# A two-layer graph attention kernel: layer 2's factor rows leave TensorE, and its node steps are put at other places

## The chip, the core and the metric

The kernel runs on one NeuronCore of a Trainium2 chip. The metric is the device time of one execution in microseconds (us). The engines are PE (TensorE), DVE (VectorE), ACT (ScalarE), POOL (GpSimd) and SP (SyncE, which only issues transfers). PSUM is the accumulator memory that PE writes, eight banks of 2 KB a partition; DVE and ACT can read and write it too. SBUF is the working memory.

## What is computed

Two graph attention layers and a small dense network over N = 6250 nodes and 100,000 edges (plus one self loop a node), edges sorted by destination; the result is added to the input `x`.

```python
def gat_conv(x, src, dst, W, a_src, a_dst, bias, heads):
    h = (x @ W).reshape(n, heads, -1)
    alpha_s = (h * a_src[None]).sum(-1); alpha_d = (h * a_dst[None]).sum(-1)
    e = leaky_relu(alpha_s[src] + alpha_d[dst], 0.2)
    alpha = softmax of e over the edges of one dst
    return segment_sum(h[src] * alpha[:, :, None], dst).reshape(n, -1) + bias

h = maximum(layernorm(x), 0)
h = relu(gat_conv(h, ..., W1, heads=4))      # layer 1, 768 -> 256
h = relu(gat_conv(h, ..., W2, heads=1))      # layer 2, 256 -> 256
h = relu(h @ Wm1 + bm1)                      # 256 -> 256
out = x + (h @ Wm2 + bm2)                    # 256 -> 768
```

## The kernel before

Nodes are cut into 49 tiles of 128 (`NT`). Edges are cut into tiles of 128, four to a group; there are 196 groups (`NG`) and 98 pairs of groups (`NU`). So one node tile corresponds to four groups, or two pairs, or eight half groups. The change lies in layer 2 (about 1425 to 2570 us of the profiled span).

One group of layer 2, two halves of two edge tiles each:

- POOL issues four indirect transfers (L726, `G<-table,src_i`), each of which gathers the rows of 128 source nodes into one quarter of a buffer `G`. There are ten such buffers, and POOL is let eight groups ahead (`AHEAD`). A buffer is free again when PE has read it.
- DVE makes a one-hot matrix for the whole group (L751, 128x512), and for each half multiplies and takes the larger (L825, L827, into the scratch tensor `iota_ps`), and multiplies that into the one-hot (L828). L825 reads a *factor row*: one number for each of the 128 destination nodes of a pair of groups, the same on all partitions. It lies in PSUM as `rho_ps`.
- PE multiplies the four edge tiles' rows by the four weighted one-hots (L834, `o_ps`, summed over a pair of groups).
- After each pair DVE adds the sum to what came over from the pair before (L852, `acc`), and ACT moves the part that reaches into the next window (L861, `sum`, two instructions).

The factor rows are made on PE: `meet(t)` (L767) turns a column of `win` into a row on all partitions, two for each node tile, into two PSUM banks of their own, used in turn.

When a node tile has its sum, a Python generator `steps` (L1205 ff.) does the rest of it, a piece at a time: DVE finishes the sum (L1203, L1204 `all_`, L1215 `rden`), ACT scales it (L1218, `o`), PE turns it (L1038, `tp`), ACT adds the bias (L1044, `rT`), PE multiplies by Wm1 (L1227, four matmuls into the second half of `tp`), ACT (L1232, `mT`), PE puts the bias row into `y_ps` (L1165) and multiplies by Wm2 (L1237), DVE adds the input (L1241, `y`, twice, 384 columns each), SP stores (L1266). Both halves of `y` use one `y_ps` bank one after the other, so the products of the second half wait until DVE has added the first.

The kernel issues everything in an order written out by hand: each engine runs its instructions in the order in which the loop over groups `g` writes them, and waits only on semaphores. Two tables set the places of layer 2: `UP_AT` (the half group at which a pair's rows are summed up) and `STEPS_AT` (the half groups at which a tile's generator is moved on one `yield`). For most tiles the six places are

```python
STEPS_AT = {t: [8 * t + 19 + k for k in (1, 2, 5, 8, 11, 14)] for t in range(NT - 2)}
```

so a tile's generator is advanced over 14 half groups, and two tiles are in work at a time.

PSUM has the eight banks: `iota_ps` (one), tag "n" (two: `tp`, `y_ps` and the completed rows `missing`/`missing2` take turns), tag "o" (three: `o_ps`), "factors" (one) and "parts" (one), the last two holding the `rho_ps` rows in layer 2. A semaphore wait is set wherever two engines touch the same PSUM tensor, whichever part of it.

Ten groups of source rows are not gathered in time from memory but completed on the chip (`next_missing`, L417/L419 on PE, `next_whole`, L423 on ACT).

Of the kernel before, what the change touches and what calls it, by code (L numbers as in the profile page):

```python
# [60 lines left out]

UP_AT = {4 * u + 11: u for u in range(NU - 16)}
UP_AT.update(zip((338, 341, 344, 348, 351, 355, 358, 362, 366, 370, 373, 377, 380, 384), range(NU - 16, NU - 2)))
STEPS_AT = {t: [8 * t + 19 + k for k in (1, 2, 5, 8, 11, 14)] for t in range(NT - 2)}
STEPS_AT.update({NT - 10: [332, 333, 336, 339, 342, 344], NT - 9: [339, 340, 343, 345, 348, 351],
                 NT - 8: [345, 346, 349, 352, 355, 358], NT - 7: [352, 353, 356, 359, 361, 364],
                 NT - 6: [359, 360, 362, 365, 368, 371], NT - 5: [367, 368, 370, 373, 375, 378],
                 NT - 4: [374, 375, 376, 378, 379, 381], NT - 3: [381, 381, 382, 384, 385, 387]})

# [3 lines left out]
def kernel(  # L73
# [337 lines left out]
    def next_missing(pool, G, i, t):  # L411

        there, hit = NEXT[i], next_hit.pop((i, t))
        d = present(pool, next_ok[:, i, t:t + 1])
        next_p[i, t] = ps.tile([P, NW[2]], F32, name="missing2", tag="n")
        for T in range(there, NT):
            nc.tensor.matmul(next_p[i, t], hit[:, T - there], kept[T][:, :NW[2]], start=(T == there),  # L417
                             stop=False)
        nc.tensor.matmul(next_p[i, t], d, G[next_pair[i] // 2][:, 2 + t, :NW[2]], start=False, stop=True)  # L419
# [5 lines left out]
    def next_steps(g, pool, G):  # L425

        for i, at in enumerate(NEXT_GROUP):
            if g == at - 10:
                next_sources(pool, i)
            for t in range(2):  # L430
                first = at - 6 + 4 * t
# [4 lines left out]
                if g == first + 1:  # L436
                    next_whole(G, i, t)

    edges_stack.enter_context(tc.manual_schedule())
# [247 lines left out]
    def layer_edges(layer, H, node, pre, matched, pre_pool):  # L687
# [4 lines left out]
        with tc.tile_pool(name=f"eg{layer}", bufs=6) as eg, \  # L692
# [5 lines left out]
            if layer == 1:  # L698
                bank = ps.tile([P, 4 * P], F32, name="factors", tag="factors", bufs=1)
                factors, rest_ps = bank[:, :2 * 16 * 3 * H], bank[:, 2 * 16 * 3 * H:]  # L700
                factors = factors.rearrange("p (s t k) -> p s t k", s=2, t=16)
                node.keep_own(pre.own, rest_ps)
            else:
                u_ps = mine_ps[:, :2 * P].rearrange("p (t n) -> p t n", t=2)
                rho_ps = [ps.tile([P, 2, P], F32, name="rho_ps", tag=tag, bufs=1)
                          for tag in ("factors", "parts")]

            def tiles(g):

# [51 lines left out]
            def meet(t):  # L761

                if t >= NT:
                    return
                if layer == 2:
                    for u in (2 * t, 2 * t + 1):
                        nc.tensor.transpose(rho_ps[t % 2][:, u % 2],  # L767
                                            pre.win[:, 2 * u + 2].to_broadcast([P, P]), ident)
# [28 lines left out]
            def group(g, first, n, one_by_one=False):  # L797
# [14 lines left out]
                        hw[:, of], Gg[:, :, :RW[1]].rearrange("p t (h c) -> p t h c", h=H),  # L812
                        w.unsqueeze(3).to_broadcast([P, n, H, C + 1]))
                else:
                    row, e1, e2 = rho_ps[u // 2 % 2][:, u % 2], Gg[:, :, HID:HID + 1], Gg[:, :, HID + 2:NW[2]]
# [95 lines left out]
            gathered = AHEAD  # L911
            matched()
            meet(0)
            if layer == 2:
                meet(1)
            if layer == 1:
                parts_out(0)
            join(0)
# [43 lines left out]

            for g in range(NG):
                t, j = divmod(g, 4)
                if layer == 2 and g >= NG - 2:
                    if g == NG - 2:
                        last_pairs()
                    continue
# [46 lines left out]
                    next_places(g - 100)  # L1015
                if g < NG - 1:
                    pair(g, 1)
                if layer == 2 and j == 3:
                    meet(t + 2)
                advance(g, 1)  # L1020
                if j == 3:
                    if layer == 1:
# [98 lines left out]
    with tc.tile_pool(name="wmp", bufs=1) as wp, tc.tile_pool(name="x3", bufs=3) as xp, \  # L1121
# [6 lines left out]
        half = OUT_DIM // 2  # L1128
        pre2 = SimpleNamespace()
        bad_i = const.tile([1, 1], I32, name="bad_i")  # L1130

        def matched():

            vars(pre2).update(vars(prepare(pre, 2, 1)))
            nc.scalar.dma_start(wm1, Wm1.rearrange("(k p) f -> p k f", p=P))
# [31 lines left out]

        class Node2:
            xs = {}

            def fetch(self, i):
                both = xp.tile([P, 2, IN_DIM], F32, name="xt", tag="xt")
# [34 lines left out]
            def steps(self, t, sum_, most=None, last=None):  # L1207
# [8 lines left out]
                yield 1  # L1216
                o = wk.tile([P, HID], F32, name="o")
                nc.scalar.activation(o, all_[:, :HID], AF.Copy, scale=rden)  # L1218
                p, m_ps = ps.tile([P, 2, KH, P], F32, name="tp", tag="n").rearrange("p s k n -> s p k n")
                turn(o, p)  # L1220
                if t == NT - 1:
                    y_pss = [start_y(s, last=True) for s in range(2)]
# [13 lines left out]
                def product(y_ps, s, j):  # L1236
                    nc.tensor.matmul(y_ps, mT[:, j], wm2[:, j, s * half:(s + 1) * half],  # L1237
                                     start=False, stop=(j == KH - 1))

                def add_x(y_ps, s):  # L1240
                    nc.vector.tensor_add(y[:n, s], y_ps[:n], xt[:n, s * half:(s + 1) * half])  # L1241

                if t == NT - 1:
# [9 lines left out]
                if t == NT - 2:  # L1253
                    yield 1
# [6 lines left out]
                if t == NT - 2:  # L1261
                    yield 1
                product(y_ps, 1, 1)
                yield 1
# [321 lines left out]
```

## Time and profile before

| what | value |
|---|---|
| median of three runs | 2570.27 us (2564.79 to 2573.91) |
| the profiled execution's own time | 2571.73 us |
| its span, first to last instruction | 2570.0 us |
| mean granted clock of PE | 0.83 of full speed |
| busy over the span: PE, DVE, ACT, POOL | 1841.2, 1522.7, 688.0, 1519.7 us |

The profile has one execution. Its timeline gives, for each group of instructions, the start and the length in us, the engine, the line, the operation, what is written and read with the shape, a count, and in brackets how long the engine had been idle and what ended that ("remote": a release that the profile can't place; "issue": nothing that it shows).

### The profile page before, as it was taken

The numbers are of one execution on the slowest core, as the hardware profiler recorded it, in microseconds if no ns is written. First come the engines' busy times: TensorE is split into PE (matmuls) and PEld (weight loads), VectorE is DVE, ScalarE is ACT, GpSimd is POOL, SyncE is SP. The second block draws the span as 40 slices with busy tenths as digits, with TensorE's granted clock in tenths as the row PEclk, the third lists the DMA queues.
The fourth block names the chain that finished last, engine by engine and source line by source line (L and its number), as shares of the span: only waits on it lengthen the run. The fifth ranks groups of instructions, "written<-read, shape, count | busy, mean of one in ns | idle before, by whom it ended". The sixth has DMA issues, their size and how long they took to land. (4 is left out here: it accounts for less than half of the span.)

```text
span 2570.0 us, 25346 instructions
## 1 busy us (share of the span) xinstructions
PE 1841.2 (72%) x7650; PEld 1362.0 (53%) x7651; DVE 1522.7 (59%) x3261; ACT 688.0 (27%) x1676; POOL 1519.7 (59%) x1742
## 2 busy tenths in 40 slices
PE   9861876867768778777766457777777667777667
PEld 7741655745656556666644235555445444544444
DVE  7631553545546555555555447766777676777675
ACT  6642332333323233333332011111111111111111
POOL 6357555556555555665564766666666666666660
PEclk9985888878878888888877668888888888888788
DMA  9976433334434444444332634444454444444441
GB/s 335 312 245 212 130 114 108 105 114 137 125 108 137 118 117 135 125 122 139 117 106 77 195 91 145 136 128 139 135 147 126 148 131 129 146 136 137 123 135 60
DMA packets 136216, 361.34 MB, mean 141 GB/s; under 512 B 32952, under 2 KB 51983, under 8 KB 132999
## 3 DMA queue, kind: packets, MB, share of 16 engines
q0 software_dynamic: 75040, 217.70, 30.8%
q1 hardware_dynamic: 59672, 140.56, 15.5%
q10 hardware_dynamic: 1358, 1.38, 0.2%
q8 instruction: 63, 1.03, 0.2%
q14 instruction: 83, 0.67, 0.1%
HBM read 316.15 MB, written 43.36 MB: 140 GB/s over the span
## 5 line engine op out<-in xcount | busy, mean ns | idle before, releaser
L726 POOL DMA_INDIRECT G<-table,src_i x1490 | 1409.3, 946 | 929.8 <-issue 406.1
L834 PE MATMUL o_ps<-G,hot 128*128 128x258 f32 x1564 | 457.2, 434 | 112.0 <-issue 50.3
L834 PE MATMUL o_ps<-hw,hot 128*128 128x260 f32 x1564 | 431.3, 416 | 86.7 <-issue 73.5
L834 PEld LDWEIGHTS o_ps<-G,hot 128*128 128x128 f32 x1564 | 321.8, 216 | 245.3 <-issue 79.7
L811 DVE TENSOR_TENSOR hw<-G,factors 128x1040 f32<-128x1040 f32 (+1 forms) x198 | 242.3, 1224 | 311.6 <-remote 184.6
L359 PE MATMUL missing<-kept,soon_hit 128*128 128x268 f32 x1280 | 353.3, 429 | 102.1 <-issue 80.2
L834 PEld LDWEIGHTS o_ps<-hw,hot 128*128 128x128 f32 x1564 | 314.4, 206 | 166.2 <-issue 109.8
L359 PEld LDWEIGHTS missing<-kept,soon_hit 128*128 128x128 f32 x1280 | 267.7, 211 | 174.3 <-issue 110.0
L861 ACT ACTIVATE sum<-acc 32x260 f32<-32x260 f32 (+1 forms) x384 | 160.0, 417 | 486.5 <-DVE acc L852 243.2
L751 DVE TENSOR_TENSOR hot<-iota_ps,dcol 128x512 f32<-128x512 f32 x392 | 265.9, 680 | 0.0
L825 DVE TENSOR_TENSOR iota_ps<-rho_ps,G 128x256 f32<-128x256 f32 x390 | 168.5, 432 | 59.5 <-ACT G L423 19.3
L1237 PE MATMUL y_ps<-wm,mT 128*128 128x384 f32 x392 | 185.0, 602 | 11.7 <-ACT mT L1232 9.9
L827 DVE TENSOR_TENSOR iota_ps<-iota_ps,G 128x256 f32<-128x256 f32 x390 | 168.5, 432 | 19.6 <-DVE iota_ps L825 5.4
L828 DVE TENSOR_TENSOR hot<-hot,iota_ps 128x256 f32<-128x256 f32 x390 | 163.9, 420 | 19.9 <-DVE iota_ps L827 4.8
L1237 PEld LDWEIGHTS y_ps<-wm,mT 128*128 128x128 f32 x392 | 77.7, 220 | 161.7 <-issue 130.4
L506 PE MATMUL h_ps<-w,r 128*128 128x264 f32 (+1 forms) x588 | 142.2, 395 | 25.2 <-ACT r L496 23.5
L1241 DVE TENSOR_TENSOR y<-y_ps,xt 128x384 f32<-128x384 f32 (+1 forms) x98 | 54.2, 554 | 171.2 <-remote 94.0
L340 DVE TENSOR_TENSOR soon_hit<-soon_of,iota_ps 128x1408 f32<-128x1408 int32 (+20 forms) x54 | 93.2, 1725 | 80.5 <-remote 68.3
L506 PEld LDWEIGHTS h_ps<-w,r 128*128 128x128 f32 x588 | 110.5, 195 | 47.7 <-ACT r L496 25.1
L366 ACT ACTIVATE G<-missing 128x268 f32<-128x268 f32 x54 | 21.1, 392 | 411.3 <-PE missing L361 181.6
L740 ACT ACTIVATE mask<-drow,less_p 128x1024 bf16<-128x1024 bf16 x98 | 112.9, 1152 | 8.3 <-issue 8.2
L742 ACT ACTIVATE mask<-mask,ones_c 128x1024 bf16<-128x1024 bf16 x98 | 112.3, 1146 | 3.2
(445 smaller groups left out, 1592.9 us busy)
## 6 DMA issues: line engine op xcount, KB each, us to landing
drow<-dmod_d SPq DMA_DIRECT2D x24, 1024.0 KB
G<-table,src_i POOLq DMA_INDIRECT x1490
xt<-in_x SPq DMA_DIRECT2D x48, 384.0 KB
xt<-in_x SPq DMA_DIRECT2D x24, 768.0 KB
out<-y SPq DMA_DIRECT2D x48, 384.0 KB
xTt<-in_xT SPq DMA_DIRECT2D x40, 384.0 KB
table<-kept SPq DMA_DIRECT2D x98, 136.0 KB
soon_d<-G SPq DMA_DIRECT2D x27, 272.0 KB
```

The costliest lines, as they stand in the source:

```text
L359: nc.tensor.matmul(soon_p[k], hit[:, T - there], kept[T][:, :NW[1]], start=(T == there), stop=False)
L506: nc.tensor.matmul(h_ps[:, :n], r[:, k], w1[:, k, :n], start=(k == 0), stop=(k == KI - 1))
L726: nc.gpsimd.indirect_dma_start(out=G[g][:n, t], out_offset=None, in_=table[layer], in_offset=bass.IndirectOffsetOnAxis(ap=src_i[:n, k:k + ...
L740: nc.scalar.activation(mask[u][:, a:b], drow[u // 4][:, at + a:at + b], AF.Abs, bias=less_p)
L751: nc.vector.tensor_tensor(hot[g][:, T[0]:T[0] + n], iota_ps.unsqueeze(1).to_broadcast([P, n, P]), dcol[:, k:k + n].unsqueeze(2).to_broadca ...
L811: nc.vector.tensor_mul(hw[:, of], Gg[:, :, :RW[1]].rearrange("p t (h c) -> p t h c", h=H), w.unsqueeze(3).to_broadcast([P, n, H, C + 1]))
L825: nc.vector.tensor_mul(u_ps[:, :m], row.unsqueeze(1).to_broadcast([P, m, P]), b.to_broadcast([P, m, P]))
L827: nc.vector.tensor_max(u_ps[:, :m], u_ps[:, :m], a.to_broadcast([P, m, P]))
L828: nc.vector.tensor_mul(hot[g][:, k:k + m], hot[g][:, k:k + m], u_ps[:, :m])
L834: nc.tensor.matmul(o_ps[u], hot[g][:, k], r, start=(g % 2 == 0 and k == 0), stop=(g % 2 == 1 and k == tiles(g)[-1]))
L861: nc.scalar.activation(done[t][r], acc[r], AF.Copy)
L1237: nc.tensor.matmul(y_ps, mT[:, j], wm2[:, j, s * half:(s + 1) * half], start=False, stop=(j == KH - 1))
```

## The change

- Layer 2's factor rows are no longer turned on PE for each node tile. `win` is turned once, stored to memory (`rho_d`), and loaded back on all partitions, eight rows (512 KB) at a time (`fetch_rho`, issued by ACT, 13 loads). From there ACT copies one row for each pair of groups into PSUM (L965, at the top of every even group). Only the first two rows still come from PE.
- One PSUM bank instead of two holds the factor rows. It is one tensor of four 128-column parts: two hold the rows in turn, and the other two (`node.spun`) take what was `tp` (the turned `o`, and in the same place the Wm1 products `m_ps`).
- The bank "parts" that this frees takes `missing2`, whose steps get a half-group pair more between product and copy.
- The two "n" banks now hold both halves of `y_ps` at once. The generator of a tile has seven pieces at half groups 1, 2, 5, 9, 10, 16, 17: `mT` at 9, all four products at 10, the two additions at 16 and 17.

```diff
-STEPS_AT = {t: [8 * t + 19 + k for k in (1, 2, 5, 8, 11, 14)] for t in range(NT - 2)}
+STEPS_AT = {t: [8 * t + 19 + k for k in (1, 2, 5, 9, 10, 16, 17)] for t in range(NT - 2)}
...  (the last eleven tiles have lists of their own, `at[:4] + at[3:]` of the six places)
-        next_p[i, t] = ps.tile([P, NW[2]], F32, name="missing2", tag="n")
+        next_p[i, t] = ps.tile([P, NW[2]], F32, name="missing2", tag="parts", bufs=1)
...
-                rho_ps = [ps.tile([P, 2, P], F32, name="rho_ps", tag=tag, bufs=1)
-                          for tag in ("factors", "parts")]
+                bank = ps.tile([P, 2 + KH, P], F32, name="rho_ps", tag="factors", bufs=1)
+                rho_ps, node.spun = bank[:, :2], bank[:, 2:]
...
             for g in range(NG):
                 t, j = divmod(g, 4)
+                if layer == 2 and g % 2 == 0 and 1 < g // 2 + 1 < NU:
+                    nc.scalar.activation(rho_ps[:, (g // 2 + 1) % 2], node.rho_row(g // 2 + 1), AF.Copy)
...
-                if layer == 2 and j == 3:
-                    meet(t + 2)
...
+        def fetch_rho(k):
+            n = min(8, NU - 8 * k)
+            if n > 0:
+                rho_rows[k] = pre.tile([P, 8, P], F32, name="rho_rows", bufs=2)
+                nc.scalar.dma_start(rho_rows[k][:, :n].rearrange("p u n -> p (u n)"), bcast(rho_d, n * P, 8 * k * P))
...
-                p, m_ps = ps.tile([P, 2, KH, P], F32, name="tp", tag="n").rearrange("p s k n -> s p k n")
+                p = m_ps = self.spun
...
-                y_ps = start_y(0)
...
-                for j in range(KH):
-                    product(y_ps, 0, j)
-                yield 1
-                add_x(y_ps, 0)
-                start_y(1, y_ps)
-                product(y_ps, 1, 0)
...
+                    yield 1
+                    y_pss = [start_y(s) for s in range(2)]
+                    for j in range(KH):
+                        for s in range(2):
+                            product(y_pss[s], s, j)
+                    yield 1
+                    add_x(y_pss[0], 0)
                 yield 1
-                add_x(y_ps, 1)
+                add_x(y_pss[1], 1)
```

Lines shift: after the change the DVE instructions that were L751, L825, L827, L828, L852, L1241 are L753, L826, L828, L829, L853, L1260; on PE L834, L1038, L1227, L1165, L1237 are L835, L1037, L1246, L1179, L1256; on ACT L861, L1044, L1232 are L862, L1043, L1251.

DVE, in the middle of layer 2, where one node tile's outputs are added. What each instruction waits for stands in brackets, one name for each engine or DMA queue (DMASW: POOL's gathers, DMAHW: the other transfers). Before:

```order
L751 TENSOR_TENSOR hot<-iota_ps,dcol 128x512
L825 TENSOR_TENSOR iota_ps<-rho_ps,G 128x256 [waits DMASW5_49,DMASW4_49,DVE_49]
L827 TENSOR_TENSOR iota_ps<-iota_ps,G 128x256 [waits DVE_49]
L828 TENSOR_TENSOR hot<-hot,iota_ps 128x256 [waits DVE_49]
L825 TENSOR_TENSOR iota_ps<-rho_ps,G 128x256 [waits DMASW7_49,DMASW6_49,DVE_49]
L827 TENSOR_TENSOR iota_ps<-iota_ps,G 128x256 [waits DVE_49]
L828 TENSOR_TENSOR hot<-hot,iota_ps 128x256 [waits DVE_49]
L1241 TENSOR_TENSOR y<-y_ps,xt 128x384 [waits DMAHW0_49,PE_49]
```

After, the same engine over two groups, from the second half of one to the first multiplication of the group after the next:

```order
L829 TENSOR_TENSOR hot<-hot,iota_ps 128x256 [waits DVE_49]
L753 TENSOR_TENSOR hot<-iota_ps,dcol 128x512
L826 TENSOR_TENSOR iota_ps<-rho_ps,G 128x256 [waits DMASW0_49,DMASW1_49,DVE_49,PE_49]
L828 TENSOR_TENSOR iota_ps<-iota_ps,G 128x256 [waits DVE_49]
L829 TENSOR_TENSOR hot<-hot,iota_ps 128x256 [waits DVE_49]
L826 TENSOR_TENSOR iota_ps<-rho_ps,G 128x256 [waits DMAHW4_49,DVE_49,Activation_49]
L828 TENSOR_TENSOR iota_ps<-iota_ps,G 128x256 [waits DVE_49]
L829 TENSOR_TENSOR hot<-hot,iota_ps 128x256 [waits DVE_49]
L853 SCALAR_TENSOR_TENSOR acc<-acc,keep,o_ps 128x258
L753 TENSOR_TENSOR hot<-iota_ps,dcol 128x512
L826 TENSOR_TENSOR iota_ps<-rho_ps,G 128x256 [waits DMASW2_49,DVE_49,DMASW3_49,PE_49,Activation_49]
```

The y additions lose their wait on PE (after, they read `L1260 TENSOR_TENSOR y<-y_ps,xt 128x384`, with no wait or one on a DMA). The first multiplication of a half, which waited on no engine but its own, waits on PE twice for each node tile: once in the group after the y products, for L1037, and once in the next group, for L1246.

PE at the same place, before: two of a tile's four y products stand behind the turn of the next tile, two elsewhere.

```order
L834 MATMUL o_ps<-G,hot 128x258 [waits DMASW4_49,DVE_49]
L834 MATMUL o_ps<-G,hot 128x258 [waits DMASW5_49]
L1038 MATMUL tp<-ident,o 128x128 [waits Activation_49]
L1038 MATMUL tp<-ident,o 128x128
L1165 LDWEIGHTS ones_r
L1165 MATMUL y_ps<-bm2r,ones_r 128x384 [waits DVE_49]
L1237 MATMUL y_ps<-wm_9105,mT 128x384 x2
L834 MATMUL o_ps<-G,hot 128x258 [waits DMASW6_49,DVE_49]
L834 MATMUL o_ps<-G,hot 128x258 [waits DMASW7_49]
```

After: all four y products in one stretch, ahead of the turn.

```order
L835 MATMUL o_ps<-G,hot 128x258 [waits DMASW6_49,DVE_49]
L835 MATMUL o_ps<-G,hot 128x258 [waits DMASW7_49]
L1179 LDWEIGHTS ones_r
L1179 MATMUL y_ps<-bm2r,ones_r 128x384
L1179 LDWEIGHTS ones_r
L1179 MATMUL y_ps<-bm2r,ones_r 128x384
L1256 MATMUL y_ps<-wm_9105,mT 128x384 [waits Activation_49]
L1256 MATMUL y_ps<-wm_9105,mT 128x384
L1256 MATMUL y_ps<-wm_9105,mT 128x384 [waits Activation_49]
L1256 MATMUL y_ps<-wm_9105,mT 128x384
L1037 MATMUL rho_ps<-ident,o 128x128 [waits Activation_49]
L1037 MATMUL rho_ps<-ident,o 128x128
```

In the name column `rho_ps` now stands for the whole shared bank. ACT, one pair of groups, after: the row copy stands between the sums and `rT`, and writes the same bank.

```order
L862 ACTIVATE sum<-acc 32x258 [waits DVE_49]
L862 ACTIVATE sum<-acc 32x258
L965 ACTIVATE rho_ps<-rho_rows 128x128 [waits PE_49]
L1043 ACTIVATE rT<-rho_ps,bT_103 128x128 [waits Activation_49]
L1043 ACTIVATE rT<-rho_ps,bT_103 128x128
```

Before, the sums are followed at once by `rT` (`L1044 ACTIVATE rT<-tp,bT_103 128x128`), which waits on PE.

More of the change, by code (lines that the diff above doesn't have):

```diff
@@ L63 @@
 UP_AT.update(zip((338, 341, 344, 348, 351, 355, 358, 362, 366, 370, 373, 377, 380, 384), range(NU - 16, NU - 2)))
-STEPS_AT = {t: [8 * t + 19 + k for k in (1, 2, 5, 8, 11, 14)] for t in range(NT - 2)}
-STEPS_AT.update({NT - 10: [332, 333, 336, 339, 342, 344], NT - 9: [339, 340, 343, 345, 348, 351],
+STEPS_AT = {t: [8 * t + 19 + k for k in (1, 2, 5, 9, 10, 16, 17)] for t in range(NT - 2)}
+STEPS_AT.update({t: at[:4] + at[3:] for t, at in {
+                 NT - 11: [324, 325, 328, 332, 337, 338],
+                 NT - 10: [332, 333, 336, 339, 342, 344], NT - 9: [339, 340, 343, 345, 348, 351],
                  NT - 8: [345, 346, 349, 352, 355, 358], NT - 7: [352, 353, 356, 359, 361, 364],
                  NT - 6: [359, 360, 362, 365, 368, 371], NT - 5: [367, 368, 370, 373, 375, 378],
-                 NT - 4: [374, 375, 376, 378, 379, 381], NT - 3: [381, 381, 382, 384, 385, 387]})
+                 NT - 4: [374, 375, 376, 378, 379, 381], NT - 3: [381, 381, 382, 384, 385, 387]}.items()})
 @with_exitstack
@@ L430, in next_steps @@
             for t in range(2):
-                first = at - 6 + 4 * t
+                first = at - 6 + 3 * t
                 if g == first - 1:
@@ L435, in next_steps @@
                     next_missing(pool, G, i, t)
-                if g == first + 1:
+                if g == first + 2:
                     next_whole(G, i, t)
@@ L765, in meet @@
                 if layer == 2:
-                    for u in (2 * t, 2 * t + 1):
-                        nc.tensor.transpose(rho_ps[t % 2][:, u % 2],
-                                            pre.win[:, 2 * u + 2].to_broadcast([P, P]), ident)
+                    for u in (0, 1):
+                        nc.tensor.transpose(rho_ps[:, u], pre.win[:, 2 * u + 2].to_broadcast([P, P]), ident)
                     return
@@ L814, in group @@
                 else:
-                    row, e1, e2 = rho_ps[u // 2 % 2][:, u % 2], Gg[:, :, HID:HID + 1], Gg[:, :, HID + 2:NW[2]]
+                    row, e1, e2 = rho_ps[:, u % 2], Gg[:, :, HID:HID + 1], Gg[:, :, HID + 2:NW[2]]
                     if one_by_one:
@@ L913, in layer_edges @@
             meet(0)
-            if layer == 2:
-                meet(1)
             if layer == 1:
@@ L1130 @@
         bad_i = const.tile([1, 1], I32, name="bad_i")
+        rho_d = dram.tile([NU, P], F32, name="rho_d")
+        rho_rows = {}
+        def fetch_rho(k):
[3 more added lines that the diff above has]
+                nc.scalar.dma_start(rho_rows[k][:, :n].rearrange("p u n -> p (u n)"), bcast(rho_d, n * P, 8 * k * P))
         def matched():
             vars(pre2).update(vars(prepare(pre, 2, 1)))
+            turned = ps.tile([NU, P], F32, name="rho_t", tag="n")
+            nc.tensor.transpose(turned, pre2.win[:, 2:NG + 2:2, 0], ident)
+            rho_t = pre.tile([NU, P], F32, name="rho_t")
+            nc.scalar.activation(rho_t, turned, AF.Copy)
+            nc.scalar.dma_start(rho_d, rho_t)
+            fetch_rho(0)
             nc.scalar.dma_start(wm1, Wm1.rearrange("(k p) f -> p k f", p=P))
@@ L1169, with rho_row @@
             xs = {}
+            def rho_row(self, u):
+                if u % 8 == 2:
+                    fetch_rho(u // 8 + 1)
+                return rho_rows[u // 8][:, u % 8]
             def fetch(self, i):
@@ L1251, in steps @@
                     return
-                y_ps = start_y(0)
                 if t == NT - 2:
+                    y_pss = [start_y(0)] * 2
                     yield 1
-                for j in range(KH):
-                    product(y_ps, 0, j)
-                yield 1
-                add_x(y_ps, 0)
-                start_y(1, y_ps)
-                product(y_ps, 1, 0)
-                if t == NT - 2:
-                    yield 1
-                product(y_ps, 1, 1)
-                yield 1
-                add_x(y_ps, 1)
+                    for j in range(KH):
+                        product(y_pss[0], 0, j)
+                    yield 1
+                    add_x(y_pss[0], 0)
+                    start_y(1, y_pss[1])
+                    product(y_pss[1], 1, 0)
+                    yield 1
+                    product(y_pss[1], 1, 1)
+                else:
+                    yield 1
+                    y_pss = [start_y(s) for s in range(2)]
+                    for j in range(KH):
+                        for s in range(2):
+                            product(y_pss[s], s, j)
+                    yield 1
+                    add_x(y_pss[0], 0)
+                yield 1
+                add_x(y_pss[1], 1)
                 nc.sync.dma_start(out[t * P:t * P + n], y[:n].rearrange("p s f -> p (s f)"))
```

## The prediction

> **What bounds the kernel now.** The change touches only layer 2, so I first asked for busy time in its even middle, 1560 to 2460 us. Columns: window, length, then busy us and count for PE, its weight loads, DVE, ACT and POOL, then PE's clock, DMA share, GB/s; the second row is the y additions (L1241) alone on DVE.
>
> ```profile
> 1560.00:2460.00 900.00, 653.14 (x2374) 447.11 (x2373) 632.50 (x1419) 147.68 (x398) 588.00 (x622) 0.85 0.46 136
> 1560.00:2460.00 900.00, 44.82 (x81) 0.85 0.46 136
> ```
>
> 81 additions are 40.5 node tiles, so a tile takes 900 / 40.5 = 22.2 us. No engine is full. The waits of DVE and POOL in the same window (total us, times, longest) say why:
>
> ```profile
> DVE y L1241 <- remote: 84.7, 16, 9.0
> DVE y L1241 <- PE y_ps L1237: 41.2, 11, 5.7
> DVE y L1241 <- PE tp L1038: 16.0, 4, 6.1
> DVE y L1241 <- PE o_ps L834: 9.9, 3, 6.6
> ...
> POOL G L726 <- issue: 150.0, 481, 3.0
> POOL G L726 <- remote: 73.8, 25, 3.9
> POOL G L726 <- PE o_ps L834: 54.4, 41, 3.4
> ```
>
> DVE stands 84.7 + 41.2 + 16.0 + 9.9 = 151.8 us in front of y additions, 3.75 us a tile. POOL's gathers come every 1.25 us while it has free buffers, and it pauses where a buffer isn't free:
>
> ```profile
> 1902.79 0.95 POOL L726 DMA_INDIRECT G<-table,src_i  x1 [0.30 <-issue]
> 1904.04 0.95 POOL L726 DMA_INDIRECT G<-table,src_i  x1 [0.30 <-issue]
> 1908.26 0.95 POOL L726 DMA_INDIRECT G<-table,src_i  x1 [3.27 <-PE o_ps L834]
> ```
>
> Sixteen gathers a tile at 1.25 us make 20.0 us, POOL's floor. DVE's floor comes from one tile's timeline, between two waits:
>
> ```profile
> 1896.11 0.42 DVE L828 TENSOR_TENSOR hot<-hot,iota_ps 128x256 f32<-128x256 f32 x1
> 1901.58 0.56 DVE L1241 TENSOR_TENSOR y<-y_ps,xt 128x384 f32<-128x384 f32 x1 [5.05 <-remote]
> 1902.05 0.68 DVE L751 TENSOR_TENSOR hot<-iota_ps,dcol 128x512 f32<-128x512 f32 x1
> ...
> 1905.43 0.47 DVE L852 SCALAR_TENSOR_TENSOR acc<-acc,keep,o_ps 128x258 f32<-128x258 f32 x1
> ...
> 1917.59 0.42 DVE L828 TENSOR_TENSOR hot<-hot,iota_ps 128x256 f32<-128x256 f32 x1
> 1922.49 0.56 DVE L1241 TENSOR_TENSOR y<-y_ps,xt 128x384 f32<-128x384 f32 x1 [4.49 <-remote]
> ```
>
> From 1901.58 to 1917.59 + 0.42 = 1918.01 DVE does a whole tile without a stop: 16.4 us. So 22.2 = 16.4 of work + 3.75 before y + about 2.0 of other waits. Now PE around the same wait:
>
> ```profile
> 1891.70 1.14 PE L834 MATMUL o_ps<-G,hot 128*128 128x258 f32 x4 [0.25 <-issue]
> 1892.77 0.33 PE L1165 MATMUL y_ps<-bm2r,ones_r 3*128 3x384 bf16 x1
> 1893.03 1.56 PE L1237 MATMUL y_ps<-wm,mT 128*128 128x384 f32 x4
> ...
> 1897.56 0.38 PE L1038 MATMUL tp<-ident,o 128*128 128x128 f32 x2
> 1902.19 0.32 PE L1165 MATMUL y_ps<-bm2r,ones_r 3*128 3x384 bf16 x1 [4.25 <-issue]
> 1902.43 2.88 PE L1237 MATMUL y_ps<-wm,mT 128*128 128x384 f32 x4
> ...
> 1908.80 1.16 PE L1227 MATMUL tp<-rT,wm 128*128 128x128 f32 x8 [1.16 <-issue]
> ```
>
> The products were over at 1893.03 + 1.56 = 1894.59, yet the addition started at 1901.58, 7 us later, though DVE was free from 1896.53. PE's completions reach DVE late in this stage, in some tiles. ACT shows the same: `rT` at 1908.13 needs the turn that ended at 1897.94, and ACT was free from 1906.77.
>
> ```profile
> 1905.93 0.84 ACT L861 ACTIVATE sum<-acc 32x258 f32<-32x258 f32 x2 [12.17 <-DVE iota_ps L827]
> 1908.13 0.62 ACT L1044 ACTIVATE rT<-tp,bT 128x128 f32<-128x128 f32 x2 [1.35 <-PE o_ps L834]
> ...
> 1928.84 0.40 ACT L348 ACTIVATE present<-ident,next_ok 128x128 f32<-128x128 f32 x1
> ```
>
> So what matters is where DVE has to wait for PE, and how much room there is before it.
>
> **The change, part by part.**
>
> *Turns of the factor rows leave PE.*
>
> ```profile
> L825 DVE TENSOR_TENSOR iota_ps<-rho_ps,G 128x256 f32<-128x256 f32 x390 | 168.5, 432 | 59.5 <-ACT G L423 19.3 <-DMA G<-table,src_i 12.7 <-remote 6.3
> ...
> L767 PE MATMUL rho_ps<-ident,win 128*128 128x128 f32 x98 | 19.8, 288 | 2.8 <-ACT win L653 2.8
> ```
>
> This is 19.8 us of PE, which is 653 of 900 busy and waits for DVE and ACT at the places above: worth nothing on the path (at most 19.8). The row above it is DVE's multiplication by the factor row: 59.5 us idle over 390, none of it named as PE.
>
> *Loads and copies of rows.* 13 loads of 512 KB are 6.7 MB beside 136 GB/s at a DMA share of 0.46, each issued six pairs (over 60 us) ahead; hidden. The first of them is used in the fifth group, 30 us after `win` is there (1415.23 to 1445.87, below), so the start costs nothing either; if store and load took longer, a few us once.
>
> ```profile
> 1415.23 0.37 ACT L653 ACTIVATE win<-rho 32x196 f32<-32x196 f32 x1
> ...
> 1445.87 0.43 DVE L825 TENSOR_TENSOR iota_ps<-rho_ps,G 128x256 f32<-128x256 f32 x1
> ```
>
>  Of the 96 row copies the trace has none. Nearest are ACT's 128x128 forms: half of `rT` (0.31) and L348 (0.40). I take 0.35; 34 us in all, on an engine busy 148 of 900. They cost only where they stand in a chain, below.
>
> *y additions later, in two banks.* The products stand at half group 10, the additions at 16 and 17, three groups behind, and in the order they no longer wait on PE. I take the 3.75 us a tile as gone.
>
> *The shared bank.* This is the new cost. DVE's multiplication reads its factor row from the bank into which PE turns `o` and multiplies by Wm1, and the order makes it wait for both, once each a tile, directly behind the PE work in question, without room.
>
> Wait (a), in the group after the products. When DVE has made the last weighted one-hot, PE still has: the half's o_ps products (1892.77 - 1891.70 = 1.07), two bias rows (0.26 each, start to start), twice the two products of the 1.56 row (3.12), the turn (0.38). That is 5.1 us; meanwhile DVE only makes the next one-hot (0.68). Stall 4.4 us. Queued behind it on DVE are the group's weighted one-hots, for which PE waits in turn, so nothing fills the gap.
>
> Wait (b), in the next group. From the end of `acc`: two sums 0.84, the row copy 0.35, `rT` 0.62, the Wm1 products 1.16, four hand-overs; 3.0 to 3.1 us. DVE has again the one-hot of 0.68. Stall 2.4 us (2.35 by the copy's lower end, 2.45 by its upper).
>
> DVE also waits for `mT` on ACT once a tile, behind sums, copy and `mT` (0.84 + 0.35 + 0.62 = 1.8 us after `acc`); DVE has an addition, the finished sum and a one-hot in between, 0.56 for the addition and 1.8 for the rest (1913.43 to 1915.23 below): nothing.
>
> ```profile
> 1913.43 0.48 DVE L1203 TENSOR_SCALAR iota_ps<-kept,own 128x258 f32<-128x258 f32 x1
> ...
> 1914.56 0.67 DVE L751 TENSOR_TENSOR hot<-iota_ps,dcol 128x512 f32<-128x512 f32 x1
> ```
>
>
> [...]
>
> *Completed rows.* `missing2` in its own bank: ACT waits less there, which nobody on the path waits for. Nothing.
>
> *The sum.* DVE a tile: 16.4 + 4.4 + 2.4 = 23.2 us, before any late completion, against 22.2 now with all of them. To this come other waits: of the 2.0 us now, which are the finished sum waiting behind late ACT work, I keep half, 1.0; and lateness at (a) and (b). The y waits have met it in 34 of 81 cases with 151.8 / 34 = 4.5 us each, 1.9 us a wait, with room of several half groups before them; at (a) and (b) there is no room, but a completion that is late by less than the stall isn't added to it. Two waits give 0 to 3.75; I take 0.5, near the low end, because a tile of over 24 us leaves POOL, with 20.0 of its own, pausing longer, and `rT` at 1908.13 was released within such a pause (1904.99 to 1908.26); the two y additions quoted were not, so this is a choice and not a finding. Together 24.7 us. From 1437 to 2460 there are 1023 / 22.2 = 46 tiles: 46 x 2.5 = +115 us. The last eleven tiles have tighter places and I count them with the rest. Against the profiled execution's own 2571.73 (span 2570.0, 1.7 outside it; 1.5 over the median of the runs) this gives about 2685 us.
>
> **The rivals.**
>
> *Bank waits cost less than DVE gains: faster.* For this stall (a) would have to be partly over when DVE arrives, say because PE does bias rows and products while DVE is still at the last half's multiplications (they wait for `mT` only), though they stand behind that half's products in order. For it: PE has room (653 of 900). It decides from a + b + rest below 22.2 - 16.4 = 5.8 us a tile. With POOL's floor of 20.0 and half the distance, 21 us: 2572 - 46 x 1.2 = 2517. By full prompt hand-overs 20.0: 2471. Against: PE runs in order, and (a) alone is 4.4.
>
> *The stalls take the place of the y waits exactly: same.* a + b + rest = 5.8 within 0.15. Possible, as 6.8 + 1.0 is an estimate with an error of about 2.
>
> *Completions late at both waits: much slower.* If each wait adds 1.9 us on top, a tile takes 24.2 + 3.75 = 28 us, 2572 + 46 x 5.8 = 2838. For it: ACT's `mT`, which has no room either, waited up to 18 us for a release that the profile can't place; against: POOL's pauses.
>
> ```profile
> ACT mT L1232 <- remote: 161.7, 16, 18.0
> ```
>
>
> *The PE turn didn't matter and the bank waits are absorbed by POOL:* if POOL's pauses were the real limit at 22.2, DVE's stalls would fill its present idle time and nothing would change; counted with "same". Against: POOL waits for buffers that PE frees after DVE.
>
> **How the numbers follow.** Slower as summed (2600 to 2760): 0.62. Much slower (over 2760): 0.14. Same: 0.06. Faster: 0.18. A measurement of this kernel can tell about 0.3%, 8 us, from no change. Range: 0.1 left out on each side: below, half of the faster cases, so 2520; above, part of the much slower, so 2810. The likeliest case's own range is 2618 (23.2 a tile, nothing late, no rest) to 2760.
>
> **What would show it.** The DVE rows of L826 carry idle time from PE, some 300 us in all in layer 2, where L825 has 59.5 now; the two rows a tile that carry it stand in the group after the y products and the next. L1260 has almost no wait. Products of y run at 1.56 us for four records, since PE comes straight from o_ps. POOL's waits on PE grow. A tile takes 24 to 25 us. I am wrong if L826's idle stays under 150 us, or if it waits 5 us and more at both places.

## The result and the profile after

The changed kernel is slower: 2727.63 us median against 2569.67 us in the same set, ratio 1.0625 (95% interval 1.058 to 1.067), +158 us. The profiled execution took 2722.92 us with a span of 2721.1. The forecast was 2685, slower.

The sets of experiments below fell on two conditions. In some the kernel before takes about 2565 us and the other engines see many of PE's completions late (3 to 12 us), as in the profile before; in others it takes 2075 us and they are seen 0.04 to 0.1 us after its end. I call these late and prompt sets; every ratio is against the kernel before in the same set.

Busy time of the layer-2 stretch 1560 to 2610 us, the y additions (now L1260) alone on DVE:

```profile
1560.00:2610.00 1050.00, 44.95 (x82) 0.80 0.41 123
```

82 additions are 41 tiles, so a tile takes 25.6 us where it took 22.2. Between 1437 and 2460 there were 46 tiles: 46 x 3.4 = 156 us, nearly the whole difference. PE's granted clock fell from 0.85 to 0.80. DVE's waits in this stretch (total us, times, longest):

```profile
DVE iota_ps L826 <- PE rho_ps L1037: 142.2, 23, 8.1
DVE iota_ps L826 <- PE rho_ps L1246: 99.2, 37, 4.2
DVE iota_ps L826 <- issue: 82.7, 14, 8.0
DVE iota_ps L826 <- remote: 43.2, 6, 8.9
```

There is one place left where DVE stands: L826, the multiplication by the factor row. The y additions no longer appear. Over the whole run, with count, busy us, mean ns, idle us before and what ended it, the lines that answer to L825 and L1241, and between them the new row copy:

```profile
L826 DVE TENSOR_TENSOR iota_ps<-rho_ps,G 128x256 f32<-128x256 f32 x390 | 168.5, 432 | 475.3 <-PE rho_ps L1037 155.5 <-PE rho_ps L1246 112.9 <-issue 89.6
...
L965 ACT ACTIVATE rho_ps<-rho_rows 128x128 f32<-128x128 f32 x96 | 25.8, 269 | 57.2 <-DVE iota_ps L826 22.4 <-DMA bm1c<-in_bm 15.8 <-issue 13.6
...
L1260 DVE TENSOR_TENSOR y<-y_ps,xt 128x384 f32<-128x384 f32 (+1 forms) x98 | 53.8, 550 | 10.2 <-PE y_ps L1256 10.1
```

The y additions' idle time fell from 171.2 to 10.2 us, that of the multiplication rose from 59.5 to 475.3. Some of these waits carry the names "issue" or "remote"; going by the semaphore that each L826 waits for, and taking the idle time before it, the 41 waits for L1037 (stall (a)) average 6.37 us and the 40 for L1246 (stall (b)) 2.78 us. 16.4 us of work + 6.37 + 2.78 = 25.6, the tile.

One tile of (a), PE and then DVE:

```profile
2124.82 1.14 PE L835 MATMUL o_ps<-G,hot 128*128 128x258 f32 x4 [0.25 <-DVE hot L829]
2129.30 1.14 PE L835 MATMUL o_ps<-G,hot 128*128 128x258 f32 x4 [3.35 <-DVE iota_ps L828]
2130.69 2.09 PE L835 MATMUL o_ps<-G,hot 128*128 128x258 f32 x4 [0.25 <-DVE hot L829]
2132.71 0.81 PE L1179 MATMUL y_ps<-bm2r,ones_r 3*128 3x384 bf16 x2
2133.46 4.84 PE L1256 MATMUL y_ps<-wm,mT 128*128 128x384 f32 x8
2138.13 0.38 PE L1037 MATMUL rho_ps<-ident,o 128*128 128x128 f32 x2
```

```profile
2125.54 0.55 DVE L1260 TENSOR_TENSOR y<-y_ps,xt 128x384 f32<-128x384 f32 x1
...
2130.22 0.42 DVE L829 TENSOR_TENSOR hot<-hot,iota_ps 128x256 f32<-128x256 f32 x1
2130.55 0.68 DVE L753 TENSOR_TENSOR hot<-iota_ps,dcol 128x512 f32<-128x512 f32 x1
2138.55 0.43 DVE L826 TENSOR_TENSOR iota_ps<-rho_ps,G 128x256 f32<-128x256 f32 x1 [7.31 <-PE rho_ps L1037]
```

DVE makes the last weighted one-hot (until 2130.64) and the next plain one, and then waits until the turn ends at 2138.51; the signal comes 0.04 us later. In front of the turn stand the half's products, the two bias rows and the four y products (eight records, two for each product). Those take 4.84 us here; in other tiles they take 2.85:

```profile
2106.83 2.85 PE L1256 MATMUL y_ps<-wm,mT 128*128 128x384 f32 x8
```

In 22 of the 41 tiles the y products take 4.6 to 5.3 us, at a mean granted clock of 0.53 to 0.61; in the other 19 they take 2.85 at a clock of 1.0. Most of the slow ones follow a stretch like the one at 2125.96 to 2129.30, in which PE has nothing to do for 3.35 us: DVE is busy there with both y additions and the finished sum. What goes with the half clock in these tiles stands at `e11` below. POOL waits longer for its buffers, behind the slower DVE (215.1 us in 1050, before 54.4 in 900):

```profile
POOL G L728 <- PE o_ps L835: 215.1, 70, 8.4
```

### The profile page after: what moved, and what is told of

Its sections match the earlier page's. It is cut to its first block, busy times and chain, and to the rows that moved or that the text cites. A ratio compares the mean times of both kernels' runs of the same rounds, so it can differ in the third digit from the quotient of the medians.

```text
span 2721.1 us, 25285 instructions
## 1 busy us (share of the span) xinstructions
PE 1944.7 (71%) x7555; PEld 1398.7 (51%) x7556; DVE 1518.9 (56%) x3261; ACT 707.5 (26%) x1773; POOL 1519.6 (56%) x1742
## 5 line engine op out<-in xcount | busy, mean ns | idle before, releaser
L835 PE MATMUL o_ps<-G,hot 128*128 128x258 f32 x1564 | 546.9, 495 | 352.8 <-DVE hot L829 244.5
L835 PEld LDWEIGHTS o_ps<-G,hot 128*128 128x128 f32 x1564 | 349.2, 239 | 516.4 <-DVE hot L829 318.4
L835 PE MATMUL o_ps<-hw,hot 128*128 128x260 f32 x1564 | 425.0, 413 | 78.5 <-issue 70.5
L826 DVE TENSOR_TENSOR iota_ps<-rho_ps,G 128x256 f32<-128x256 f32 x390 | 168.5, 432 | 475.3 <-PE rho_ps L1037 155.5
L361 PE MATMUL missing<-kept,soon_hit 128*128 128x268 f32 x1280 | 360.8, 435 | 95.2 <-issue 76.5
L862 ACT ACTIVATE sum<-acc 32x260 f32<-32x260 f32 (+1 forms) x384 | 160.0, 417 | 980.5 <-DVE acc L853 826.8
L835 PEld LDWEIGHTS o_ps<-hw,hot 128*128 128x128 f32 x1564 | 312.8, 204 | 149.6 <-issue 94.4
L753 DVE TENSOR_TENSOR hot<-iota_ps,dcol 128x512 f32<-128x512 f32 x392 | 265.9, 680 | 0.0
L1256 PE MATMUL y_ps<-wm,mT 128*128 128x384 f32 x392 | 194.8, 657 | 1.1 <-ACT mT L1251 1.1
L828 DVE TENSOR_TENSOR iota_ps<-iota_ps,G 128x256 f32<-128x256 f32 x390 | 168.6, 432 | 18.4 <-DVE iota_ps L826 3.1
L829 DVE TENSOR_TENSOR hot<-hot,iota_ps 128x256 f32<-128x256 f32 x390 | 164.0, 420 | 18.5 <-DVE iota_ps L828 4.3
L1256 PEld LDWEIGHTS y_ps<-wm,mT 128*128 128x128 f32 x392 | 96.3, 258 | 87.8 <-issue 65.7
L508 PEld LDWEIGHTS h_ps<-w,r 128*128 128x128 f32 x588 | 110.6, 195 | 40.5 <-ACT r L498 20.4
L775 PE MATMUL e_parts<-win,mask 128*128 128x12 bf16 x782 | 33.1, 169 | 105.7 <-issue 54.8
```

What stands on the lines that cost most here:

```text
L361: nc.tensor.matmul(soon_p[k], hit[:, T - there], kept[T][:, :NW[1]], start=(T == there), stop=False)
L508: nc.tensor.matmul(h_ps[:, :n], r[:, k], w1[:, k, :n], start=(k == 0), stop=(k == KI - 1))
L753: nc.vector.tensor_tensor(hot[g][:, T[0]:T[0] + n], iota_ps.unsqueeze(1).to_broadcast([P, n, P]), dcol[:, k:k + n].unsqueeze(2).to_broadca ...
L826: nc.vector.tensor_mul(u_ps[:, :m], row.unsqueeze(1).to_broadcast([P, m, P]), b.to_broadcast([P, m, P]))
L828: nc.vector.tensor_max(u_ps[:, :m], u_ps[:, :m], a.to_broadcast([P, m, P]))
L829: nc.vector.tensor_mul(hot[g][:, k:k + m], hot[g][:, k:k + m], u_ps[:, :m])
```

## The experiments

My theory after the result: the shared bank alone costs the time; DVE's two waits are as long as the PE and ACT work that stands in front of them; and (a) is longer than I summed because PE's clock is halved at the y products in half the tiles. Rivals: late completions go with whatever DVE waits for; sharing costs as much wherever the products stand; the half clock comes from elsewhere.

The sets are `e1` to `e4` (prompt), `e5` to `e8` (late) and `e9` to `e12` (prompt); the first result belongs to a late one. The expectations of the later sets speak of a slower and a faster chip; see the last section for why that was not it.

**e1: the same, without sharing.**

```diff
-                bank = ps.tile([P, 2 + KH, P], F32, name="rho_ps", tag="factors", bufs=1)
-                rho_ps, node.spun = bank[:, :2], bank[:, 2:]
+                rho_ps = ps.tile([P, 2, P], F32, name="rho_ps", tag="factors", bufs=1)
...
-                y_ps = ps.tile([P, half], F32, name="y_ps", tag="n")
+                y_ps = y_banks[s][:, :half]
...
-                p = m_ps = self.spun
+                if not y_banks:
+                    y_banks.extend(ps.tile([P, 4 * P], F32, name="y_bank", tag="n") for _ in range(2))
+                p = m_ps = [b[:, half:half + P] for b in y_banks]
```

> The changed kernel, but the turned o and the Wm1 products leave the factor rows' bank: their two 128-column halves take the free columns of the two y banks (384 of 512 used). Nothing else is moved but the second last tile, whose products come in one stretch too. Theory (the shared bank makes DVE wait, 6.4 + 2.8 = 9.2 us a tile at L826): both waits go; a tile falls from 25.6 to between POOL's 20.0 and 21.5 us, so 2727 - 46 x (4.1 to 5.6) = 2470 to 2540 us. The y additions now wait on PE again, with over 3 us of room. Rival (late completions of PE go with whatever DVE waits for): the y additions take up 3.75 us a tile as before the change, and the time is 2560 to 2590.

Two things that the lines above leave out: the second last tile's products come in one stretch, and the accumulator of a small sum (`n_ps`) goes to the bank "parts". Measured 2074.89 us, ratio 1.0003 (0.9994 to 1.0012). The set was a prompt one, so the absolute numbers of the expectation don't apply. What follows: everything else in the change (later additions, both y banks, the rows by ACT, `missing2`) together costs and gains no time here, where DVE waits for POOL's gathers (81.6 us in 1200 to 1950 us); the slowdown is the sharing. `e8` repeats it in a late set.

**e2: products one half group later.**

```diff
-STEPS_AT = {t: [8 * t + 19 + k for k in (1, 2, 5, 9, 10, 16, 17)] for t in range(NT - 2)}
+STEPS_AT = {t: [8 * t + 19 + k for k in (1, 2, 5, 9, 11, 16, 17)] for t in range(NT - 2)}
```

> The changed kernel with one number moved: the four y products one half group later (11 instead of 10), so that the turn of the next tile no longer stands behind them on PE. Bank still shared. Theory (stall (a) is the products in front of the turn): (a) falls from 6.4 to about 1 us; stall (b) grows by what the products push back, 0 to 2 us; 2727 - 46 x (3.4 to 5.4) = 2480 to 2570 us. Rival (the stall is the sharing itself, whatever stands ahead of the turn): L826 keeps over 7 us a tile and the time stays above 2640.

Measured 2161.4 us, 1.0419 (1.0403 to 1.0435); the unaltered change is at 1.120 in such a set (`e9`). Stall (a) averages 1.58 us, (b) 2.76. One number in the table takes away two thirds of the loss: (a) is what stands on PE ahead of the turn. In the repeat (`e10`, 1200 to 2000 us) DVE's waits are

```profile
DVE iota_ps L826 <- PE rho_ps L1246: 95.7, 34, 4.7
DVE iota_ps L826 <- PE rho_ps L1037: 59.6, 33, 2.3
```

**e3: additions two half groups earlier.**

```diff
-STEPS_AT = {t: [8 * t + 19 + k for k in (1, 2, 5, 9, 10, 16, 17)] for t in range(NT - 2)}
+STEPS_AT = {t: [8 * t + 19 + k for k in (1, 2, 5, 9, 10, 14, 15)] for t in range(NT - 2)}
```

> The changed kernel with the two y additions at half groups 14 and 15 instead of 16 and 17. They leave the stretch in which DVE finishes a tile's sum and PE stands idle 3.3 us just ahead of the y products. Theory (that idle time halves PE's clock, and the products then run at 4.7 to 5.2 us instead of 2.7): the stretch shrinks to about 2.4 us, the products run at 2.7 in nearly all tiles, (a) falls from 6.4 to about 4.4 us on average; 2727 - 46 x 2 = about 2635 us. Rival (the slow products come from elsewhere, the throttle or the whole stage's load): (a) stays at 6.4, 2720 to 2735.

Measured 2276.23 us, 1.0963 (1.0946 to 1.0980). (a) averages 4.66 us where about 4.4 was expected, its median is 4.05; the products are slow in 5 of 33 tiles. Read with `e9`.

**e4: the rows alone.** The kernel before, with `rho_d`, `fetch_rho` and the ACT copy at the top of even groups, one bank for the rows, and nothing else.

```diff
-                    for u in (2 * t, 2 * t + 1):
-                        nc.tensor.transpose(rho_ps[t % 2][:, u % 2],
+                    for u in (0, 1):
+                        nc.tensor.transpose(rho_ps[:, u], pre.win[:, 2 * u + 2].to_broadcast([P, P]), ident)
...
+                if layer == 2 and g % 2 == 0 and 1 < g // 2 + 1 < NU:
+                    nc.scalar.activation(rho_ps[:, (g // 2 + 1) % 2], node.rho_row(g // 2 + 1), AF.Copy)
```

> The kernel before with only the factor rows changed: stored, loaded by broadcast and copied by ACT into one bank of their own; steps, tp, y and missing2 as before. Theory (turns on PE were off the path, loads and copies are hidden): within 0.3% of before, 2562 to 2578 us. Rival (DVE waits for the row copy behind the two sums, about 0.5 us twice a tile): 2600 to 2620 us.

Measured 2075.43 us, 1.0000 (0.9991 to 1.0009). By ratio, the theory. The wait for the copy is there, and small (1200 to 1950 us); with POOL's pace as the limit it costs nothing. The same rows in a late set are in `e8`.

```profile
DVE iota_ps L823 <- DMA G<-table,src_i: 84.7, 49, 4.3
DVE iota_ps L823 <- ACT rho_ps L962: 12.6, 22, 0.6
DVE y L1257 <- PE y_ps L1253: 4.4, 9, 0.5
```

**e5: the changed kernel again.** No edit.

> The changed kernel itself, on the chip of the last four runs, where the kernel before takes 2075 us instead of 2570 and no completion of PE comes late. Theory (the shared bank's two waits, and PE's half clock at the y products): work 16.4 + (a) 6.0 to 6.6 + (b) 2.75 = about 25.5 us a tile, with products at 4.5 to 5.2 us in half the tiles; against POOL's 20.0 that is 48 x 5.5 = +260, 2310 to 2360 us, so 40 to 80 above the run with the earlier additions (2276). Rival (the half clock came with the late completions of the first chip): (a) is 4.1 to 4.7 as with the earlier additions, 2270 to 2285 us.

Measured 2729.81 us, 1.064 (1.0604 to 1.0676): a late set, and the first result over again, with (a) at 6.62 us and (b) at 2.76 (1560 to 2460 us). What was expected for the prompt condition is tested in `e9`.

**e6: the kernel before again.** No edit.

> The kernel before, for a profile on this chip. Theory (what made it 2570 us on the first chip is that PE's completions reach the others late): POOL's gathers follow one another every 1.25 us without a pause in both layers, y additions wait under 10 us in all, no completion of PE is seen over 0.3 us late, 2073 to 2077 us. Rival (another clock or slower transfers on the first chip): instructions of one form differ in length between the two chips.

2571.88 us in a single run: a late set, so it says nothing of the prompt condition. Its y waits are as in the profile before (154.9 us in 1560 to 2460).

**e7: the sharing alone.** `e4` with the bank shared; steps, y and `missing2` as before the change.

```diff
-                rho_ps = ps.tile([P, 2, P], F32, name="rho_ps", tag="factors", bufs=1)
+                bank = ps.tile([P, 2 + KH, P], F32, name="rho_ps", tag="factors", bufs=1)
+                rho_ps, node.spun = bank[:, :2], bank[:, 2:]
...
-                p, m_ps = ps.tile([P, 2, KH, P], F32, name="tp", tag="n").rearrange("p s k n -> s p k n")
+                p = m_ps = self.spun
```

> The rows by ACT copies (as in the run that equalled the kernel before) and the bank shared, but steps, y and missing2 as before the change: the turn stands ahead of two of the products, the other two stand elsewhere. Theory (the price of sharing is what PE has to do ahead of the turn and the Wm1 products): (a) falls to 0.4 to 1 us, (b) stays 2.7; 16.4 + 3.1 to 3.7 = 19.5 to 20.1 us a tile, just POOL's 20.0: 2070 to 2110 us. Rival (sharing costs 9 us wherever the products stand): 2280 and more. If this lands on the slower chip: 2600 to 2660 by the theory, 2700 and more by the rival.

Measured 2589.02 us, 1.0101 (1.0070 to 1.0131), in a late set: the theory's side, a little under its range. DVE now waits at the multiplication instead of at y (1560 to 2460 us):

```profile
DVE iota_ps L824 <- remote: 125.0, 25, 13.2
DVE iota_ps L824 <- PE rho_ps L1244: 55.3, 21, 4.3
DVE iota_ps L824 <- PE rho_ps L1035: 18.7, 22, 2.6
...
DVE y L1258 <- PE y_ps L1254: 6.4, 8, 1.3
```

By semaphore, (a) is 1.60 us a tile and (b) 3.88, of which 2.7 us together are late signals. So in a late set the sharing is dear only together with the new place of the products. What it costs alone in a prompt set wasn't run; there `e2`, with the products behind the turn, still loses 4.2%.

**e8: without sharing, again.** The kernel of `e1`.

> The same as the earlier run without sharing, to have it beside the changed kernel and the one before in one set. On the chip of the last runs 2073 to 2077 us (POOL's gathers bound it). If this lands on the slower chip: 2470 to 2540 us if the later additions escape the late completions, 2560 to 2590 if they don't.

Measured 2566.77 us, 1.0004 (0.9972 to 1.0036), in a late set. Here the rival was right: the additions, six half groups behind their products, still wait (1560 to 2460 us),

```profile
DVE y L1263 <- remote: 73.0, 14, 7.3
DVE y L1263 <- PE y_bank L1249: 60.6, 13, 7.3
DVE y L1263 <- PE o_ps L834: 48.8, 20, 6.7
```

though in this kernel they wait for the last PE write of the y bank, which is the next tile's Wm1 products (L1249), three half groups ahead. So it doesn't tell whether the whole distance would have escaped the late signals.

**e9: the changed kernel in a prompt set.** No edit.

> The changed kernel once more, in one set with the next two, since the sets so far ran on two chips (before: 2570 us on one, 2075 us on the other). On the slower chip 2720 to 2735 us again, 25.6 us a tile. On the faster one: by the theory (half clock at the y products belongs to the order, not to the chip) 2310 to 2360 us with (a) at 6.0 to 6.6 us; by its rival (it belongs to the slower chip) 2270 to 2285 us with (a) at 4.1 to 4.7.

Measured 2325.14 us, 1.1203 (1.1184 to 1.1221). The theory by the time, and (a) a little under its 6.0 to 6.6 us but well over the rival's 4.7. The waits (1200 to 2000 us) have their true names, since nothing comes late, and a tile takes 800 / 32 = 25.0 us:

```profile
DVE iota_ps L826 <- PE rho_ps L1037: 182.8, 32, 8.2
DVE iota_ps L826 <- PE rho_ps L1246: 81.1, 30, 3.5
```

(a) is 182.8 / 32 = 5.71 us, (b) 2.67. The products are slow (over 4 us from the first product to the turn) in 12 of 32 tiles, against 5 of 33 in `e3`, and the time is 49 us above `e3`.

**e10: e2 again.** The kernel of `e2`.

> The changed kernel with the products one half group later. On the faster chip 2161 us as before. On the slower one, theory (the two waits are 1.6 and 2.8 us, which fit into the 5.8 us a tile that DVE idles there anyway): 2560 to 2610 us, near the kernel before. Rival (waits add to what there is): 2570 + 46 x (20.8 - 20.0) and the late completions, 2650 us and more.

2163.73 us, 1.0428 (1.0410 to 1.0445): a prompt set, as `e2`. What it does in a late set wasn't measured.

**e11: e3 again.** The kernel of `e3`.

> The changed kernel with the two additions two half groups earlier. On the faster chip 2276 us as before. On the slower one, theory (half clock comes from PE's idle 3.3 us ahead of the products): (a) falls from 6.4 to 6.6 to about 4.7 to 5.2 us, 2640 to 2680 us. Rival (the half clock comes from elsewhere there): 2715 to 2735.

2275.54 us, 1.0964 (1.0946 to 1.0983), beside 1.1203 for the change in the same set. PE's rows in this kernel:

```profile
1539.43 1.14 PE L835 MATMUL o_ps<-G,hot 128*128 128x258 f32 x4 [2.42 <-DVE hot L829]
1540.82 1.14 PE L835 MATMUL o_ps<-G,hot 128*128 128x258 f32 x4 [0.25 <-DVE hot L829]
1541.89 0.49 PE L1179 MATMUL y_ps<-bm2r,ones_r 3*128 3x384 bf16 x2
1542.31 2.85 PE L1256 MATMUL y_ps<-wm,mT 128*128 128x384 f32 x8
1545.00 0.38 PE L1037 MATMUL rho_ps<-ident,o 128*128 128x128 f32 x2
```

The idle time ahead is 2.42 us instead of 3.35, and the products take 2.85. Counted over the three profiles of the changed kernel, by the longest idle time of PE in the 6 us before the bias rows: with 3 us or more, 54 of 65 tiles have slow products (over 4 us), with less, 5 of 49. In `e3` and `e11` no tile has 3 us, and 10 of 66 are slow.

So the length of the idle time doesn't decide alone. In the clock records of the changed kernel's profile the granted clock is 1.0 or 0.5. In all 22 slow tiles of the first profile and all ten of `e3` and `e11`, PE was busy for 23 to 47% of the 3.41 us before its clock fell to 0.5. Here are the 3.41 us before that for the tile above, and the 3.42 us after, in which the slow products start, in the changed kernel's profile (columns as in the prediction, PE's busy time first and its clock third from the end):

```profile
2127.27:2130.68 3.41, 1.14 (x4) 0.68 (x4) 3.15 (x8) 0.73 (x3) 2.50 (x4) 1.00 0.93 374
2130.68:2134.10 3.42, 3.41 (x7) 1.80 (x8) 0.56 (x1) 0.00 (x0) 2.51 (x3) 0.50 0.60 200
```

An idle stretch of 3.35 us was also followed by products at full speed: before those at 2029.01 us, 2.85 us long, the clock was 0.50 from 2024.87 to 2028.28 and 1.00 in the 3.42 us from there. In the ten slow tiles of `e3` and `e11` an idle stretch under 3 us was enough. What else sets the clock no run here shows.

**e12: POOL six groups ahead.** The kernel before.

```diff
-AHEAD = 8
+AHEAD = 6
```

> The kernel before with POOL let six groups ahead instead of eight, and eight buffers G instead of ten (in both layers). Theory (on the slower chip a tile's 22.2 us is set by late completions of PE that release POOL's buffers, so DVE's waits are a part of that and not a sum of their own): a layer-2 tile takes 23 us or more there, POOL pauses longer, and the whole takes 2620 us or more. Rival (DVE's waits set the tile, POOL only follows): a tile stays at 22.2 us and the time within 1% of 2570. On the faster chip both expect 2073 to 2085 us.

2074.31 us in a single run, a prompt set, where both views expect the same: it decides nothing about the late condition. It shows that in the prompt condition two buffers can be spared; POOL waits 0.3 us at the longest (1200 to 1950 us):

```profile
1501.11 0.95 POOL L726 DMA_INDIRECT G<-table,src_i  x1 [0.30 <-issue]
1502.36 0.95 POOL L726 DMA_INDIRECT G<-table,src_i  x1 [0.30 <-issue]
1503.61 0.94 POOL L726 DMA_INDIRECT G<-table,src_i  x1 [0.30 <-issue]
```

The kernels side by side, tile time from the count of y additions in the window, stalls by semaphore:

| kernel | condition | ratio | us a tile | (a) | (b) |
|---|---|---|---|---|---|
| before | late | 1 | 22.2 | - | - |
| no sharing (e8) | late | 1.0004 | 22.5 | - | - |
| sharing alone (e7) | late | 1.0101 | 22.5 | 1.60 | 3.88 |
| changed | late | 1.0625 | 25.6 | 6.37 | 2.78 |
| rows alone (e4) | prompt | 1.0000 | 19.5 | - | - |
| no sharing (e1) | prompt | 1.0003 | 19.2 | - | - |
| products later (e2) | prompt | 1.0419 | 21.1 | 1.58 | 2.76 |
| additions earlier (e11) | prompt | 1.0964 | 24.2 | 4.49 | 2.79 |
| changed (e9) | prompt | 1.1203 | 25.0 | 5.71 | 2.67 |

No version beat the kernel before in either condition.

## Why the prediction was right, and where its steps were off

**The mechanism held.** DVE waits at L826 twice a tile, for the turn and for the Wm1 products, because they share the factor rows' bank; without the sharing the loss is gone in both conditions (`e1`, `e8`). The kernel's waits hold for the whole shared tensor, whichever columns of it are written, and here that cost 158 us; no run shows what happens without them.

**The turns, the loads and the copies: nothing.** Right (`e4`, 1.0000 in a prompt set; `e8`, which has the same rows, 1.0004 in a late one). A copy took 0.27 us, under both ends of my bound (0.31 to 0.40).

**y waits gone: right of the place, wrong as a term.** They went (171.2 to 10.2 us). But I read 22.2 = 16.4 + 3.75 + 2.0 as a sum in which each part could be taken out. In the late condition `e6`, `e7` and `e8` keep 22.2 to 22.5 us a tile and DVE's idle time keeps 230 to 237 us in 900, whether it stands before y, before the multiplication, or at the finished sum. So in that condition about 5.8 us of waits a tile could change places without changing the time. That stalls are absorbed is what my fourth rival said; I had given it part of 0.06. It did not decide because the two stalls together are 9.15 us. My rival's cause, POOL's pauses, doesn't fit the traces: in `before`, `e6`, `e7` and `e8` DVE waits for gathers 0 to 2.5 us in 900, where `e1` and `e4` have 81.6 and 84.7 in 750, and in `before` each gather was issued 36 to 50 us ahead of the multiplication that reads it (in `e4` 2.8 to 8.7). POOL waits there for the others, and not they for it. `e12` was to test it and fell into the other condition; what holds the tile at 22.2 us stays open. POOL's own 20.0 us was a little high too: not every group is gathered, and the window's 620 gathers for 40.5 tiles are 15.3 a tile, 19.1 us at 1.25 (`e1` takes 19.2 a tile); it entered only the prices of the rivals.

**Stall (a): the mis-sized term.** Summed 4.4, measured 6.37. In the 19 tiles of the first profile whose products ran at full clock it averages 4.68 us, of which 1.10 are late signals; in `e3` and `e11`, without late signals, the median is 4.05. The rest is the step where I took the products at 1.56 us for four records "since PE comes straight from o_ps": in the other 22 tiles they ran near half speed, 4.6 to 5.3 us for all eight records instead of 2.85, and the o_ps products ahead of them in part with them (1.7 to 2.1 instead of 1.14), and (a) averages 7.82. These tiles make 22 x (7.82 - 4.4) / 41 = 1.8 of the 2.0 us that were missing. The new places put both additions, the finished sum and a one-hot between two halves on DVE, PE is idle 3.3 us, and in the slow tiles the granted clock falls to 0.5 between 1.9 and 6.6 us before the products start (0.53 to 0.61 over them). I had quoted such a row (4.25 us idle, then 2.88 for four records) and not looked for a new idle stretch. The idle time alone would not have told it: in the slow tiles PE was busy for 23 to 47% of the 3.41 us before the clock fell. Moving the additions out took 49 us.

**Stall (b).** Summed 2.4, measured 2.78: two sums, copy and `rT` as expected, but the Wm1 products too ran at half speed for some or all of their time in 14 of 41 tiles (1.6 to 2.1 us instead of 1.16).

**Late completions and the rest.** I added 0.5 us for late signals at (a) and (b); the parts of these waits that lie behind the end of the PE work are (23.5 + 10.1) / 41 = 0.8 us, and they are within the two stalls as measured. The 1.0 us of other waits that I kept was 0: the work and the two stalls make up the whole tile.

**The sum.** 24.7 us forecast, 25.6 measured; +115 forecast, +158 measured. The difference of 0.9 us x 46 = 41 us is (a) + 2.0 and (b) + 0.4, less the 0.5 + 1.0 that I had added apart. That the total came out so near is partly luck: without the 1.5 us that were not there, the stalls alone would have left it 2.4 x 46 = 110 us short.

**What would show it.** L826 idle 475 us instead of "some 300", L1260 almost none, POOL's waits on PE grown: as said. A tile of 24 to 25 us: 25.6, a little more. Products at full clock: wrong in 22 of 41 tiles.

## What to carry to other kernels

Before two things share an accumulator bank, list for each reader what the writer's engine has in its queue ahead of that write: here the reader waited for all of it (6.37 and 2.78 us a tile), and a multiplication that had waited on no engine but its own became a point where two engines take turns. Where such a wait can't be avoided, put the long work behind the write and not ahead of it (here one number in a table, two thirds of the loss in a prompt set). And when steps are gathered at one place on one engine, look how long that leaves TensorE idle: in the 32 slow tiles of `after`, `e3` and `e11` its clock fell to 0.5 after 3.41 us in which it had been busy for 23 to 47%, and the work that fell into the half clock was just what the other engine waited for.

## What was not expected of the hardware

The same kernel takes 2075 us in some sets and 2563 to 2570 in others, with instructions of the same length (the plain one-hot 679 and 680 ns, a gather 0.95 us every 1.25). In the prompt sets the others see PE's completions 0.04 to 0.1 us after its end, and POOL's gathers wait 0.3 us at the longest (`e1`, `e4` and `e12`, 1200 to 1950 us). In the late sets many come 3 to 12 us late: of 37 y additions that waited in `e6` (1560 to 2460 us), 28 started over 1 us after the products' end, and 8 of these waited on no engine but PE and on no transfer. The late profiles also hold fewer records of signals: `before` has 1336 semaphore updates for the 1536 PE instructions that make one and 1832 for DVE's 3129, while `e4` has all of them, so names given to waits in a late set are less sure than in a prompt one. The records of `e1` to `e8` name the same chip, and yet the first four of them were prompt and the last four late, so it isn't the chip; what it is, no run here shows. In the changed kernel completions are late less often, even in late sets (32 of the 45 waits for the turn in layer 2 within 0.2 us), so a late set hides a part of the loss: 6.25% there, 12.0% in a prompt set.
